# Block products of the last two pairs at other points of pair 1's outputs, and GpSimd's differences of x behind a partial sum

## The chip, the cores and the metric

The kernel runs on one core of one Trainium2 chip. The metric is the device time of the whole program in microseconds (us). The engines are TensorE (PE, matmuls), VectorE (DVE, elementwise work, 32x32 transposes, reductions), ScalarE (ACT, activations and copies), GpSimd (POOL, elementwise work and some DMA issues) and SyncE (SP, DMA issues). Each engine runs its own instructions in program order and waits for the others through semaphores.

## The reference

Eight samples of 512 tokens with 256 features, each with 64 context rows; three experts; everything in float32. The part that matters:

```
nx       = layer_norm(x) * gamma + beta
q, k, v  = nx @ Wq, context @ Wk, context @ Wv
weights  = softmax(q k^T / 16)                       # over the 64 context rows
evidence = weights @ v
combined = [nx, evidence, anchor]                    # 3 x 256 features
probs    = softmax(combined @ router_W + router_b)   # 3 experts
h        = silu(combined @ e_w1 + e_b1)              # 3 x 512
routed   = sum over experts of probs * (h @ e_w2 + e_b2)
g        = sigmoid(silu(combined @ gate_w1 + gate_b1) @ gate_w2 + gate_b2)
out      = x + g * (routed @ out_w + out_b)
```

The kernel never forms `evidence`. It multiplies v with the evidence rows of the first-layer weights ("v and W", the tile `vw`), and then applies the softmax weights to that product.

## The kernel before

**Pairs.** The eight samples are taken in four pairs j = 0 to 3. A pair goes through `gate_layer(j)` (the head of the first layer), `half_layers(j)` (the first layers of gate and experts, in an order written out by hand in `SLOTS`), and `outputs(j)` (second gate layer, experts' second layer, gating, stores). Products are done as seven block products instead of eight (Winograd's scheme), with sums and differences of blocks made beforehand and added afterwards. `combine_x(j)` makes the differences of x for that: four subtractions of 128x512, on GpSimd for pairs 1 to 3 (line 682).

**Order.** All engines' instructions are in program order (`manual_schedule(engines=None)`). While pair j is in `outputs`, the next pair is prepared: the main loop puts steps into `between`, a list for each named point ("begin", "P1", "P8", "P5", "P6", "P2", "P7", "P3", "P4"), and `outputs` calls `run(point)` at these places. Between the points stand the experts' products (`experts`, twelve matmuls of 512 columns each) and the output steps: `keep` (add a partial sum from PSUM to a row sum, line 1418), `subtract` (blocks of h, line 1402), `finish` (three DVE steps, lines 1432 to 1434, one GpSimd addition of x, line 1435, and the stores). For j < 3 the order is: experts u, `keep` r11, P1, experts z, `subtract`, `keep` r22, P8, `subtract`, P5, experts u, `keep` r12, P6, experts y, `finish` r11, P2, `subtract`, experts u, `finish` r22, P7, experts z, `finish` r12, P3, experts u, `finish` r21, P4. Then comes `gate_layer(j + 1)`, with steps at points 1, 5, 6, 3 and 7 (`within`).

**v and W of the last two pairs.** JS is 2. For pairs 0 and 1, `vw` comes from ordinary products (`value_weights`). For pairs 2 and 3 together it comes from seven block products with rows of v (`block_rows`) and columns of W. Part 0 (experts 0 and 1, blocks of 512 columns) is done in `outputs(1)`, part 1 (expert 2, blocks of 256 columns) in `gate_layer(2)`. `block_columns(part)` holds the blocks of W and the three buffers for differences t1, t2 and t4; `late_difference(part, n)` makes one of four differences on DVE (line 886); `late_product(part, n, ps)` is one block product. `late_values(part, banks)` takes three PSUM banks u, y and z and returns four steps:

- first: product 1 into u, ACT copy (line 912), product 2 into y, DVE addition of y (line 907);
- second: product 6 on top of u, ACT copy (line 918);
- third: product 7 on top of u, product 5 into z, ACT copy of z (line 924), DVE addition of u (line 907);
- fourth: product 4 on top of u, ACT copy (line 929), product 3 on top of z, DVE addition of z (line 907), and for the columns finished `value_differences` (line 836).

Part 0's steps are put at P5, P6, P7 and P3 by `late_start`, which runs at P1, and so stand last in each of these lists. Part 1's differences are at P4, its steps in the gate layer at points 1, 5, 6 and 7.

**Other steps named below.** `scores` (line 691, PE), `exponents` (lines 705 to 719: DVE transpose, ACT copy of the logits, DVE maximum and scaling, ACT exponentials), `softmax` (lines 735 and 736, DVE), `evidence_logits` (lines 755 and 758, DVE), `router_logits` (lines 764 to 770, DVE), `turn_weights` (lines 743 and 745, DVE transposes), `router_exp` (line 776, ACT), `gpsimd_behind(column)` (line 125: GpSimd copies one column, and so waits for whoever writes it).

Of the kernel before, what the change touches and what calls it, by code (L numbers as in the profile page):

```python
# [16 lines left out]
def kernel(  # L17
# [53 lines left out]
    B, T, H = x.shape  # L71
# [28 lines left out]
    def bank(i, name):  # L100
        ps = psum.tile([P, 512], F32, tag=f"b{i}", name=name)
        bank_of[ps.name] = i
        return ps

    def spares(*banks):
        spare[:] = banks
# [16 lines left out]
    def gpsimd_behind(column):  # L123

        nc.gpsimd.tensor_copy(behind_t, column)
# [163 lines left out]
    mr = const.tile([P, KH, B, CT], F32, tag="mr", name="mr")  # L289
# [206 lines left out]
    ow_sb = const.tile([P, KH, H], F32, tag="ow_sb", name="ow_sb")  # L496
# [336 lines left out]
    def value_differences(j, g):  # L833
        odd = S["vw", j][CT:, g * RH : (g + 1) * RH]
        odd = odd.rearrange("p (q i c) -> p q i c", i=2, c=P)
        nc.vector.tensor_tensor(odd[:, :, 0, :], odd[:, :, 0, :], odd[:, :, 1, :], ALU.subtract)
# [3 lines left out]
    JS = NP - 2  # L840
    late_v = {}
# [19 lines left out]
    def block_columns(part):  # L861

        if part not in late_v:
            if part == 0:
                c0, n = 0, RH
                t4 = const.tile([P, RH], F32, tag="late_t4", name="late_t4")
                late_v["t4"] = t4
                ts = ow_sb.rearrange("p k n -> p (k n)"), mr[:, :, : B // 2, :], t4
            else:
                c0, n = 2 * RH, RH // 2  # L870
                ts = ow_sb[:, 0, :], ow_sb[:, 1, :], late_v["t4"][:, :n]
            w = [
                [w1[:, KH + k, c0 + i * n : c0 + (i + 1) * n] for i in range(2)] for k in range(KH)
            ]
            late_v[part] = w, ts
        return late_v[part]
# [12 lines left out]
    def late_product(part, n, ps, start=False):  # L889

        ((b11, b12), (b21, b22)), ts = block_columns(part)
        t1, t2, t4 = (t.rearrange("p k b c -> p k (b c)") if len(t.shape) > 3 else t for t in ts)
        rhs = {1: b11, 2: b21, 3: b22, 4: t4, 5: t1, 6: t2, 7: b12}[n]
        product(like(ps, rhs), block_rows(n), rhs, start)

    def late_homes(part):
        (c0, n) = (0, RH) if part == 0 else (2 * RH, RH // 2)
        first, second = S["vw", JS], w1[:, KH, :]
        return [a[:, c0 + i * n : c0 + (i + 1) * n] for a in (first, second) for i in range(2)]

    def late_values(part, banks):

        n = RH if part == 0 else RH // 2
        u, y, z = (bank(i, f"ps_late_{m}")[:, :n] for i, m in zip(banks, "uyz"))

        def plus(dst, ps):
            nc.vector.tensor_tensor(dst, dst, ps, ALU.add)

        def first():
            c11 = late_homes(part)[0]  # L910
            late_product(part, 1, u, True)
            nc.scalar.copy(c11, u)
            late_product(part, 2, y, True)
            plus(c11, y)

        def second():
            late_product(part, 6, u)
            nc.scalar.copy(late_homes(part)[1], u)

        def third():  # L920
            c22 = late_homes(part)[3]
            late_product(part, 7, u)
            late_product(part, 5, z, True)
            nc.scalar.copy(c22, z)
            plus(c22, u)

        def fourth():
            late_product(part, 4, u)
            nc.scalar.copy(late_homes(part)[2], u)
            late_product(part, 3, z)  # L930
            plus(late_homes(part)[1], z)
            for g in (0, 1) if part == 0 else (2,):
                value_differences(JS, g)

        return first, second, third, fourth

    GROUPS = (NE // 2, *range(NE // 2))
# [399 lines left out]
    def outputs(j, steps):  # L1337
        last = j == NP - 1

        def run(point):  # L1340
            for step in steps.get(point, ()):
                step()
# [15 lines left out]
        t2, t3, t4 = gate_sums.pop(j)  # L1358
        g1, g2, g22 = scratch_x("r11"), scratch_x("r12"), scratch_x("r22")
        u, z, y = (bank(i, f"ps_g{n}_{j}") for n, i in (("u", 0), ("z", 2), ("y", 4)))  # L1360
# [26 lines left out]
        def experts(ps, lhs, k, i, start=False):  # L1387
            for q in range(NQ):
                product(ps, lhs(q), hidden(j, q, k, i), start=start and q == 0)

        def combo(s):
            return lambda q: w2s[:, s, q, :]
# [24 lines left out]
        def keep(r, ps):  # L1417
            nc.vector.tensor_tensor(r, r, ps, ALU.add)
# [32 lines left out]
        def finish_late(r, ps, i, row):  # L1451
# [5 lines left out]
        r11, r22, r12, r21 = (  # L1457
            bias_sum(f"r{i + 1}{row + 1}", i, row) for i, row in ((0, 0), (1, 1), (0, 1), (1, 0))
        )
        ug = u  # L1460
        u, y, z = (bank(i, f"ps_{n}2_{j}") for i, n in ((1, "u"), (3, "y"), (5, "z")))
# [10 lines left out]
        run("P5")  # L1472
        experts(u, combo(S2), 0, 1)
        keep(r12, u)
        run("P6")
        if j + 1 < NP:
            experts(y, lambda q: a(q, 0, 1), 1, 0, start=True)
# [53 lines left out]
    with tc.manual_schedule(engines=None):  # L1531
# [77 lines left out]
        def end_setup():  # L1609
# [3 lines left out]
                anchor_columns(g)  # L1613
            value_differences(0, 2)

        for j in range(NP):


            within, between = {}, {}

            def put(where, n, step, *args):
                where.setdefault(n, []).append(lambda: step(*args))

            spares(7, 5)
            if j == 0:
                spares(4, 5, 1)
                copies = []

                def value_product(g):
                    value_weights(0, g, lambda *args: copies.append(args), False)  # L1630

                def copy_values():
                    nc.scalar.copy(*copies.pop(0))

                put(within, 1, value_product, 0)
                put(within, 1, begin_softmax)
                put(within, 5, copy_values)
                put(within, 6, load_table, AF.Silu)
                put(within, 3, value_product, 1)
                put(within, 3, copy_values)  # L1640
                put(within, "sums", end_softmax)
                put(within, 7, value_product, 2)
                put(within, 7, copy_values)
                put(within, 7, end_setup)
            elif j < JS:
                put(within, 3, value_weights, j, 1, nc.scalar.copy, False)
            elif j == JS:
                for point, step in zip((1, 5, 6, 7), late_values(1, (6, 5, 7))):
                    put(within, point, step)
            if j + 1 < NP:  # L1650
                b0, b1 = 2 * j + 2, 2 * j + 3
                if j + 2 < NP:
                    put(between, "begin", load_x, b0 + 2)
                    put(between, "begin", load_x, b1 + 2)
                put(between, "begin", transpose_blocks, b0)
                put(between, "gate", regroup_x, b1)
                put(between, "begin", value_weights, j + 1, E)
                put(between, "begin", store_router_rows, j + 1)
                put(between, "begin", spread_router_rows, j + 1)
                put(between, "P8", transpose_blocks, b1)  # L1660
                put(between, "P6", scores, j + 1)
                put(between, "P6", exponents, j + 1)
                put(between, "P6", combine_x, j + 1, nc.gpsimd)
                if j + 1 < JS:
                    put(between, "P6", value_weights, j + 1, 2)
                elif j + 1 == JS:

                    def late_start():
                        for point, step in zip(("P5", "P6", "P7", "P3"), late_values(0, (0, 2, 4))):
                            put(between, point, step)  # L1670

                    put(between, "P1", late_start)
                    for n in range(4):
                        put(between, "P4", late_difference, 1, n)
                put(between, "P7", softmax, j + 1)
                if j + 1 < JS:
                    put(between, "P7", value_weights, j + 1, 0)
                elif j + 1 > JS:
                    put(between, "P7", value_differences, j + 1, 0)
                    put(between, "P3", value_differences, j + 1, 1)  # L1680
                put(between, "P7", evidence_logits, j + 1)
                put(between, "P7", router_logits, j + 1)
                put(between, "P3", turn_weights, j + 1)
                put(between, "P3", router_exp, j + 1)
            gate_layer(j, within)
            half_layers(j)
            outputs(j, between)


# [32 lines left out]
```

## Time and profile before

| | |
|---|---|
| time, median of 3 runs | 461.32 us (460.79 to 463.81) |
| time of the profiled execution | 463.05 us |
| its span, first to last instruction | 461.2 us |
| mean granted TensorE clock | 0.996 |
| `outputs(1)`, start of the second gate layer to pair 2's gate layer | 199.04 to 255.13 us |
| `gate_layer(2)` up to the first half product | 255.13 to 265.17 us |

The busy time of an engine is the union of its instructions' spans. A matmul's record is longer than the step from one to the next, since they are pipelined: paces are taken from start to start. In a timeline, instructions of one kind in a row are merged into one line with their count, and the bracket at the end has the idle time of the engine before them and what ended it. Both sides of a line are named by tiles: `ps_late_u`, `ps_late_y` and `ps_late_z` are the three banks of the block products.

### The profile page before, as it was taken

The page shows a single profiled execution, that of the slowest core. Times are in us where ns is not written, and L with a number is a line of the kernel's source. Part 1 is how long each engine was busy: PE and PEld are TensorE (multiplying, and loading weights), DVE is VectorE, ACT ScalarE, POOL GpSimd, SP SyncE. Part 2 cuts the span into 40 slices and gives each one's busy share as a digit, 9 for nine tenths or more (in the row PEclk, how much of TensorE's full clock was granted, in tenths as well). Part 3 has the DMA queues.
Part 4 walks back from the last instruction along what each step waited for, and adds up shares of the span by engine and source line. Part 5 has one row for each costly group of instructions (what it writes and reads, how often), then busy time and mean ns, then how long its engine had stood idle before and what let it go on. Part 6 is the DMA issues. An engine that isn't in the chain of part 4 may idle for free.

```text
span 461.2 us, 5521 instructions
## 1 busy us (share of the span) xinstructions
PE 451.3 (98%) x1801; PEld 215.5 (47%) x1801; DVE 368.7 (80%) x698; ACT 214.5 (47%) x378; POOL 99.7 (22%) x149
## 2 busy tenths in 40 slices
PE   8999999999999999999997899999999999999996
PEld 6554445754444444444443444444444444444445
DVE  2878989949698998879798599857989947677983
ACT  3545875463402675474410267547440265658000
POOL 5456600342622200001521120000262220000010
PEclk9999999999999999999998999999999999999999
DMA  8975582363012478003012137500302183000004
GB/s 261 387 154 125 89 248 36 60 125 41 1 28 40 150 155 158 19 1 49 3 23 46 23 98 183 87 1 1 50 2 46 30 207 40 1 0 0 1 16 76
DMA packets 119380, 35.32 MB, mean 77 GB/s; under 512 B 106012, under 2 KB 116312, under 8 KB 118840
## 3 DMA queue, kind: packets, MB, share of 16 engines
q1 hardware_dynamic: 115344, 27.02, 28.7%
q0 software_dynamic: 2080, 7.16, 4.6%
q10 hardware_dynamic: 1928, 0.80, 0.7%
q8 instruction: 14, 0.23, 0.2%
q14 instruction: 14, 0.11, 0.1%
HBM read 27.56 MB, written 7.39 MB: 76 GB/s over the span
## 4 chain that ended last, share of the span: by engine, by line
PE 89%; DVE 5%; DMA 3%; POOL 1%; issue 0%; SPq 0%; DVEq 0%; POOLq 0%
PE ps_u L944 40%; PE ps_z L944 18%; PE ps_y L944 13%; PE ps_gu L944 3%; PE ps_vw L822 3%; PE ps_w2o L547 2%; DMA pb<-pd 2%; PE ps_s L691 2%; PE ps_gz L944 1%; PE ps_tokens L944 1%; PE ps_late_u L944 1%; DMA scr_ctx<-in_ctx_dram 1%; DVE h L1402 1%; PE ps_v L356 1%; PE ps_m L356 1%; PE ps_gy L944 1%
## 5 line engine op out<-in xcount | busy, mean ns | idle before, releaser
L944 PE MATMUL ps_u<-nxT,w 64*128 64x512 f32 (+1 forms) x208 | 96.7, 591 | 0.0
L1023 DVE TENSOR_TENSOR h<-h,pb 128x512 f32<-128x512 f32 x96 | 62.6, 685 | 16.7 <-ACT h L980 10.8
L944 PE MATMUL ps_u<-h,w2o 128*128 128x512 f32 x144 | 64.5, 597 | 0.0
L980 ACT ACTIVATE h<-h,abias 128x512 f32<-128x512 f32 x72 | 49.1, 717 | 30.5 <-DVE h L986 30.4
L944 PE MATMUL ps_y<-nxT,w 64*128 64x512 f32 (+1 forms) x104 | 51.6, 590 | 0.0
L944 PE MATMUL ps_z<-nxT,ws 64*128 64x512 f32 (+1 forms) x104 | 51.5, 591 | 0.0
L944 PE MATMUL ps_z<-T,ws 64*128 64x512 f32 (+1 forms) x104 | 51.5, 590 | 0.0
L1435 POOL TENSOR_TENSOR yb<-yb,xb 128x512 f32<-128x512 f32 x14 | 20.7, 1481 | 138.4 <-DVE yb L1434 125.3
L944 PEld LDWEIGHTS ps_u<-nxT,w 64*128 64x128 f32 (+1 forms) x208 | 37.3, 187 | 26.0 <-issue 22.9
L944 PE MATMUL ps_u<-T,ws 64*128 64x512 f32 (+1 forms) x104 | 49.4, 589 | 0.0
L944 PE MATMUL ps_u<-T,w 64*128 64x512 f32 x112 | 48.3, 590 | 0.0
L944 PEld LDWEIGHTS ps_u<-h,w2o 128*128 128x128 f32 x144 | 27.7, 193 | 33.7 <-issue 33.4
L944 PE MATMUL ps_z<-h,w2s 128*128 128x512 f32 x96 | 42.5, 592 | 0.0
L944 PE MATMUL ps_z<-wT,vw 64*128 64x512 f32 x78 | 39.2, 590 | 0.0
L989 ACT COPY h<-ps_u 128x512 f32<-128x512 f32 x48 | 27.7, 579 | 21.2 <-PE ps_u L944 20.1
L1402 DVE TENSOR_TENSOR h<-h,h 128x1024 f32<-128x1024 f32 x24 | 37.4, 1611 | 0.0
L944 PEld LDWEIGHTS ps_z<-h,w2s 128*128 128x128 f32 x96 | 18.2, 190 | 23.0 <-issue 22.0
L944 PEld LDWEIGHTS ps_y<-nxT,w 64*128 64x128 f32 (+1 forms) x104 | 19.4, 187 | 12.7 <-issue 12.4
L944 PEld LDWEIGHTS ps_z<-T,ws 64*128 64x128 f32 (+1 forms) x104 | 19.2, 187 | 12.5 <-issue 11.3
L944 PEld LDWEIGHTS ps_z<-nxT,ws 64*128 64x128 f32 (+1 forms) x104 | 19.0, 187 | 12.7 <-issue 9.8
L944 PEld LDWEIGHTS ps_u<-T,ws 64*128 64x128 f32 (+1 forms) x104 | 18.4, 187 | 13.2 <-issue 12.3
L944 PEld LDWEIGHTS ps_u<-T,w 64*128 64x128 f32 x112 | 18.3, 187 | 13.0 <-issue 12.3
(271 smaller groups left out, 850.3 us busy)
## 6 DMA issues: line engine op xcount, KB each, us to landing
pb<-pd POOLq DMA_DIRECT2D x4, 1536.0 KB, 6.8
xb<-in_x_dram SPq DMA_DIRECT2D x64, 64.0 KB, 2.4
out_dram<-yb SPq DMA_DIRECT2D x56, 64.0 KB, 1.9
x<-in_x_dram SPq DMA_DIRECT2D x24, 128.0 KB, 3.0
xd<-x SPq DMA_DIRECT2D x24, 128.0 KB, 2.5
xg<-xd SPq DMA_DIRECT2D x48, 64.0 KB, 2.2
w<-in_L_xcond_e_w_dram SPq DMA_DIRECT2D x4, 512.0 KB, 6.9
scr_wa<-in_L_xcond_e_w_dram SPq DMA_DIRECT2D x3, 512.0 KB, 9.4
```

The costliest lines, as they stand in the source:

```text
L356: nc.tensor.matmul(ps, w_sb[:, k, m * P : (m + 1) * P], src[:, k, :], start=(k == 0), stop=(k == KH - 1))
L547: nc.tensor.matmul(ps[:, d * H : (d + 1) * H], w2["T"][u % 2][:, c : c + P], ow_sb[:, k, :], start=(k == 0), stop=(k == KH - 1),)
L691: nc.tensor.matmul(ps[side(i, h), g * NH : (g + 1) * NH], mr[:, k, 2 * j + i, g * TB : (g + 1) * TB], S["nxT", 2 * j + i][:, k, h * NH : ( ...
L822: nc.tensor.matmul(ps, vT[:, k, j * 2 * CT : (j + 1) * 2 * CT], w1[:, KH + k, n0:n1], start=(k == 0), stop=(k == KH - 1),)
L944: return nc.tensor.matmul(ps, lhsT, rhs, start=start, stop=True, skip_group_check=not start)
L980: nc.scalar.activation(h, h if src is None else src, AF.Silu, bias=abias[:, c, 2 * j + i : 2 * j + i + 1])
L989: nc.scalar.copy(chunk(n, i, d), part)
L1023: nc.vector.tensor_tensor(h, h, S["pb", j][:, i, :, 2 * q // RC, :], ALU.mult)
L1402: nc.vector.tensor_tensor(d, p, m, ALU.subtract)
L1435: nc.gpsimd.tensor_tensor(yb, yb, S["xb", 2 * j + row][:, i, :], ALU.add)
```

## The change

Three things change.

1. In `outputs(1)`, the second step of part 0 stands ahead of pair 2's scores instead of at the end of P6; the third step's products and copy stand between scores and exponents at P6 instead of at the end of P7, and its DVE addition behind the exponents' DVE steps (the third step now returns it as a function); the fourth step stands at the end of P7 instead of at the end of P3. The first stays at P5. In `gate_layer(2)` the third step of part 1 is called with its addition at once.
2. Part 1's four differences are at the beginning of P3, ahead of `turn_weights`, instead of at P4. Their t4 lies in `mr` (a 128x256 part that pairs 0 and 1 used) instead of in the buffer of part 0's t4.
3. In every pair's `outputs`, GpSimd copies a column of r12 after `keep(r12, u)`, ahead of P6, so that `combine_x` comes behind that partial sum.

```diff
@@ block_columns
                 t4 = const.tile([P, RH], F32, tag="late_t4", name="late_t4")
-                late_v["t4"] = t4
...
-                ts = ow_sb[:, 0, :], ow_sb[:, 1, :], late_v["t4"][:, :n]
+                ts = ow_sb[:, 0, :], ow_sb[:, 1, :], mr[:, 0, : B // 2, :].rearrange("p b c -> p (b c)")
@@ late_values, third
             late_product(part, 5, z, True)
             nc.scalar.copy(c22, z)
-            plus(c22, u)
+            return lambda: plus(c22, u)
@@ outputs
         experts(u, combo(S2), 0, 1)
         keep(r12, u)
+        gpsimd_behind(r12[:, 0:1])
         run("P6")
@@ main loop
+        late = []
         for j in range(NP):
...
             elif j == JS:
-                for point, step in zip((1, 5, 6, 7), late_values(1, (6, 5, 7))):
-                    put(within, point, step)
+                first, second, third, fourth = late_values(1, (6, 5, 7))
+                put(within, 1, first)
+                put(within, 5, second)
+                put(within, 6, lambda third=third: third()())
+                put(within, 7, fourth)
...
                 put(between, "P8", transpose_blocks, b1)
+                if j + 1 == JS:
+                    put(between, "P6", lambda: late[1]())
                 put(between, "P6", scores, j + 1)
+                if j + 1 == JS:
+                    put(between, "P6", lambda: late.append(late[2]()))
                 put(between, "P6", exponents, j + 1)
+                if j + 1 == JS:
+                    put(between, "P6", lambda: late.pop()())
                 put(between, "P6", combine_x, j + 1, nc.gpsimd)
...
                     def late_start():
-                        for point, step in zip(("P5", "P6", "P7", "P3"), late_values(0, (0, 2, 4))):
-                            put(between, point, step)
+                        late[:] = late_values(0, (0, 2, 4))
 
                     put(between, "P1", late_start)
+                    put(between, "P5", lambda: late[0]())
                     for n in range(4):
-                        put(between, "P4", late_difference, 1, n)
+                        put(between, "P3", late_difference, 1, n)
...
                 put(between, "P7", router_logits, j + 1)
+                if j + 1 == JS:
+                    put(between, "P7", lambda: late[3]())
                 put(between, "P3", turn_weights, j + 1)
```

## The prediction

> **What bounds the kernel now.** I read the page first, then the list of waits of TensorE (PE), then busy time and clock in stretches around those waits, then the timelines of PE, VectorE (DVE) and GpSimd (POOL) there. The page:
>
> ```profile
> span 461.2 us, 5521 instructions
> ...
> PE 451.3 (98%) x1801; PEld 215.5 (47%) x1801; DVE 368.7 (80%) x698; ACT 214.5 (47%) x378; POOL 99.7 (22%) x149
> ...
> PEclk9999999999999999999998999999999999999999
> ```
>
> PE is busy 98%: the change moves PE work and takes none away, so it can gain only what PE loses in waits and at a lower clock; the one low clock digit lies in slice 22 (242.1 to 253.7 us). The waits of PE, microseconds, times, longest:
>
> ```profile
> PE ps_late_u L944 <- DVE w L907: 2.9, 1, 2.9
> PE ps_late_u L944 <- DVE ow_sb L886: 1.5, 1, 1.5
> ```
>
> The two long waits inside the kernel are both on the block products that the change touches. PE's timeline there (start, duration, [idle before]):
>
> ```profile
> 238.21 5.31 PE L944 MATMUL ps_z<-h,w2s 128*128 128x512 f32 x12
> ...
> 246.46 1.41 PE L944 MATMUL ps_late_u<-late_t,vT 128*128 128x512 f32 x2 [2.94 <-DVE w L907]
> ...
> 255.13 1.02 PE L944 MATMUL ps_u<-nxT,w 128*128 128x512 f32 x2
> ...
> 256.86 1.02 PE L944 MATMUL ps_z<-T,ws 128*128 128x512 f32 x2
> ...
> 259.41 0.67 PE L944 MATMUL ps_late_u<-ow_sb,vT 128*128 128x256 f32 x2 [1.53 <-DVE ow_sb L886]
> ...
> 265.17 0.69 PE L944 MATMUL ps_y<-wT,vw 64*128 64x512 f32 x1
> ```
>
> and stretches (busy times, then granted clock):
>
> ```profile
> 243.40:246.46 3.06, 0.12 (x1) 0.00 (x0) 2.82 (x9) 0.22 (x1) 0.00 (x0) 1.00 0.26 44
> 246.46:250.00 3.54, 3.54 (x5) 1.50 (x6) 3.37 (x6) 0.58 (x1) 1.27 (x1) 0.60 0.00 0
> 250.00:253.00 3.00, 3.00 (x8) 1.30 (x7) 2.37 (x6) 0.00 (x0) 0.00 (x0) 0.90 0.51 87
> ...
> 259.40:265.20 5.80, 5.79 (x20) 3.35 (x20) 1.98 (x5) 1.68 (x4) 0.00 (x0) 1.00 0.27 47
> ```
>
> Pace at full clock: twelve 512-column instructions from 205.25 to 210.40, 5.15 us, so 0.43 each and 0.86 for a block product (two instructions; half of it with 256 columns). PE's loss:
> - Product 4 of part 0 could start at 238.21 + 5.15 = 243.36 and starts at 246.46: 3.10.
> - From 246.46 to 255.13, 8.67 us, it runs 16 instructions worth 6.87. The granted clock there was 0.60, then 0.90, after the wait: 1.80.
> - Product 6 of part 1 could start at 256.86 + 0.86 = 257.72 and starts at 259.41: 1.69. Then 5.72 us instead of 5.59: 0.13, at a clock of 1.00.
>
> Sum 6.7 us. That is all there is to gain here; pairs 0 and 2 have no such wait in their outputs.
>
> Why PE waits, in DVE's timeline:
>
> ```profile
> 219.57 5.61 DVE L1402 TENSOR_TENSOR h<-h,h 128x1024 f32<-128x1024 f32 x3
> ...
> 231.55 0.69 DVE L1432 TENSOR_TENSOR r<-r,ps_y 128x512 f32<-128x512 f32 x1 [3.24 <-PE ps_y L944]
> ...
> 240.34 1.77 DVE L736 TENSOR_TENSOR w<-w,rs 128x512 f32<-128x512 f32 x1
> ...
> 245.73 0.68 DVE L907 TENSOR_TENSOR w<-w,ps_late_u 128x512 f32<-128x512 f32 x1
> ...
> 255.33 0.69 DVE L1432 TENSOR_TENSOR r<-r,ps_u 128x512 f32<-128x512 f32 x1 [2.87 <-PE ps_u L944]
> ...
> 257.89 1.37 DVE L886 TENSOR_TENSOR ow_sb<-w,ow_sb 128x256 f32<-128x256 f32 x1
> ```
>
> and of line 1402 alone from 219 to 226 us (shortest, median and longest ns):
>
> ```profile
> L1402 DVE TENSOR_TENSOR h<-h,h x3: 1182/2291/2293, 219.6 to 222.9; 128x1024 f32<-128x1024 f32 x3
> ```
>
> The third step's addition (245.73) stands in DVE's queue behind softmax and evidence; product 4 writes the bank that it reads. Part 1's differences (257.89) stand behind the last output's steps, though DVE had idled 2.87 us just before. The last row: DVE's two-input subtracts take 1.18 alone and 2.29 beside POOL's differences of x (POOL at 219.99 and 221.96, 1.89 and 2.14).
>
> **The change, part by part**, from the profiled execution (span 461.2, time 463.05, so 1.85 around it; it lies 1.73 above the median of the three runs, 461.32).
>
> *Third step at P6.* Products 7 and 5, 1.72 of PE, move from after the experts of "P7" to before ps_y; product 6 only trades places with the scores. No PE work is added, but everything from ps_y to the softmax slides 1.72: DVE's 231.55 becomes 233.27. ACT's copies of the second and third step stand ahead of the copy of the logits, and that one waits for product 5: products at 223.37 (6), scores 224.23 to 226.09, products 7 and 5 to 227.81, ACT's copy (0.58) to 228.5, logits' copy 0.2, DVE's maximum and scaling 1.0 to 229.7, the addition 0.7 to 230.4. DVE had been idle there (3.24 before 231.55), so this costs nothing up to 233.27; beyond, it would go one for one into DVE's queue. The exponentials, 2.8 us in all, end at about 232.7 instead of 231.3, and the softmax asks for them at 241.9. Product 4 then finds its bank read 8 us early: the 3.10 goes, and with it the 1.80 of low clock.
>
> *Fourth step at P7.* Product 4 at 238.2, product 3 to 239.9, experts to 245.1 and 250.2: pair 2's gate layer begins at 250.2 instead of 255.13. Their subtract ends at 238.16 + 1.72 = 239.9, and its first third is enough to start. On DVE the fourth step (250.98 to 252.46, 1.4 net of overlap) moves in front of the r12 output.
>
> *Part 1's differences at P3, ahead of the turning of the weights.* What is late next is DVE's queue, which now has no gap from 233.27 on. Durations are today's: up to the router's logits 247.45 (245.73 + 1.72); fourth step 1.40, 248.85; r12 output 2.13 (246.33 to 248.46), 250.98; differences 2.39 (257.47 to 259.86, a POOL addition beside them in both cases), 253.37, the second of them done at 252.77; turning 2.52 (248.46 to 250.98), 255.89; r21 output 2.14 (255.33 to 257.47), 258.03; part 1's two additions 0.41 each, 258.85. PE from 250.23: product 6 of part 1 is due at 252.81 and its difference is ready at 252.77, so the 1.69 goes; product 4 of part 1 is due at 257.54 and its bank is read at 258.85: a new wait of 1.3. Both ends: none if DVE gains 1.3 somewhere, 3.1 with a low clock as today if it is 1.8 later. I take 1.3, worked out from rows with the same neighbours.
>
> After a wait of 1.69 the clock stayed 1.00 (259.40 to 265.20), after 3.10 it fell to 0.60. 1.3 lies near the first, so I add nothing for the clock.
>
> The Trainium skill, "TensorE: Matmul & The Clock Gate", Part 1, says that the clock is judged in free-running windows of about 3.4 us, which would make the drop after a wait of 3.1 us depend on where a window falls. By that the 1.80 would be lost in some executions only, and the gain in the others would be 3.6.
>
> *Another t4 for part 1* (a quarter of mr that pairs 0 and 1 used): same instruction, same size; nothing. Product 4 of part 0 no longer shares a buffer with it. *Pair 2's gate layer*: the third step's function is called at once, so the order is the same.
>
> *GpSimd behind the partial sum.* One copy of a 128x1 column, then combine_x, in pairs 0 to 2 (pair 3 gets the copy alone). POOL's differences would start at about 224.5 instead of 219.99 and end by about 230 (1.27 to 1.34 each without a neighbour: rows at 224.98 and 226.28). Behind the waiting copy stand only they and the outputs' additions, the first at 235; their reader is the next gate layer, 20 us later. DVE's three subtracts shrink from 5.61 to about 3.4. PE waited for none of it, so 0 for the time; the price if the cover goes is in the slow rival. The small copy's length is not in the trace: between 0.1 (the smallest POOL memset seen) and 1.3, and neither matters. In P6 beside POOL now run a PSUM transpose, a maximum and additions from PSUM, and additions from PSUM took 0.67 beside POOL at 225.10.
>
> The Trainium skill, "SBUF — State Buffer", section "SBUF: two separate sides", says that GpSimd holds it for a whole instruction against DVE's two-input and two-port forms. By that the small scaling at L717 could be held up to 1.3, which DVE's gap before 233.27 hides; the sum would not change.
>
> Sum: -3.10 - 1.80 - 1.69 - 0.13 + 1.3 = -5.4: 463.05 - 5.4 = 457.65 for that execution, 461.32 - 5.4 = **455.9** on the median, 1.2% less.
>
> **Rivals.**
> 1. *DVE's queue is shorter than I add up*: no new wait, -6.7, 454.6. For: I count each POOL neighbour at today's price. Against: the queue is full. 0.10.
> 2. *The new wait lowers the clock*: -5.4 + 1.8 = -3.6, 457.7. Against: the 1.69 row. 0.15.
> 3. *The wait has only moved*: DVE 1.8 later than my sum, product 4 of part 1 waits 3.1 and the clock falls: -6.7 + 4.9 = -1.8, 459.5. For: 25 us of queue without a gap. 0.12.
> 4. *Slower*: combine_x comes beside the r11 output and the subtract after it. Four two-input steps each pay 1.1 (2.29 less 1.18): DVE +4.4, the new wait 5.7, the clock 1.8, together 7.5 against 6.7 lost now: +0.8, 462.1. It decides if POOL starts after about 228, so that its 5 us reach 233.3. Against: the partial sum is due at 224.3. 0.05.
>
> **How the numbers follow.** My forecast has 0.58. Range 454.5 to 459.5: from no new wait to the moved wait; about 0.1 lies outside, with 0.5 us of scatter on either side. 1% (4.6 us, about what a measurement tells from no change) divides at 456.7: the forecast lies 0.8 below it. Faster: 0.50 of the forecast's 0.58 and rival 1, 0.60. Slower by over 1% needs more than rival 4: 0.03. Within 1%: 0.37.
>
> **What would show it.** Right: no wait of ps_late_u on L907 near 238, clock 1.00 from 238 to 260, pair 2's gate layer near 250, a wait of about 1.3 on L907 near 258, L1402 beside no L682. Wrong: a wait over 2.5 us near 258 or a clock below 0.9 after it; a wait for ps_late at 223 to 228 (then ACT's copies are the bound); POOL's L682 after 231.

## The result, and the profile after

The changed kernel takes 458.01 us (median of 6, 457.04 to 458.82) against 461.56 for the kernel before in the same comparison (median of 6): ratio 0.9916, 95% interval 0.9889 to 0.9943. Repeated beside 10 executions of before, it took 458.44 (median of 6) against 462.85: 0.9903, 0.9886 to 0.9920. It is faster by close to 1%, inside the range and on the side that was forecast, but by 3.6 and 4.4 us, less than the forecast 5.4.

The page of the profiled execution (458.82 us):

```profile
span 456.8 us, 5532 instructions
...
PE 450.8 (99%) x1801; PEld 220.0 (48%) x1801; DVE 363.6 (80%) x698; ACT 214.5 (47%) x378; POOL 95.2 (21%) x153
...
PEclk9999999999999999999999999999999999999999
```

The digit 8 of the clock is gone. Lines 868 to 1474 of the program are one lower than before: 907 is now 906, 886 is 885, 1402 is 1401. The waits of PE:

```profile
PE ps_wake L316 <- DVE warm_t L195: 1.1, 1, 1.1
PE ps_late_u L943 <- DVE w L906: 0.9, 1, 0.9
PE ps_u L943 <- DVE h L985: 0.3, 1, 0.3
```

Both long waits (2.9 on line 907, 1.5 on line 886) are gone, and a new one of 0.9 stands on the addition of u. PE's timeline shows where:

```profile
240.30 5.31 PE L943 MATMUL ps_z<-h,w2s 128*128 128x512 f32 x12
245.45 5.31 PE L943 MATMUL ps_u<-h,w2o 128*128 128x512 f32 x12
250.60 1.02 PE L943 MATMUL ps_u<-nxT,w 128*128 128x512 f32 x2
...
252.32 1.02 PE L943 MATMUL ps_z<-T,ws 128*128 128x512 f32 x2
253.40 0.67 PE L943 MATMUL ps_late_u<-ow_sb,vT 128*128 128x256 f32 x2
...
257.35 1.02 PE L943 MATMUL ps_u<-nxT,w 128*128 128x512 f32 x2
259.31 0.70 PE L943 MATMUL ps_late_u<-mr,vT 128*128 128x256 f32 x2 [0.94 <-DVE w L906]
...
260.37 0.69 PE L943 MATMUL ps_y<-wT,vw 64*128 64x512 f32 x1
```

The experts follow each other at full pace (5.15 us from start to start), pair 2's gate layer starts at 250.60, and product 4 of part 1 starts at 259.31 where 257.35 + 0.86 = 258.21 was possible: 1.10 lost. Product 6 of part 1 starts at 253.40 where 252.32 + 0.86 = 253.18 was possible: another 0.22. DVE's timeline has the reason:

```profile
229.25 0.07 DVE L707 MEMSET w<- 128x8 f32 x1 [1.93 <-ACT lg L706]
...
230.15 0.68 DVE L906 TENSOR_TENSOR w<-w,ps_late_u 128x512 f32<-128x512 f32 x1
233.63 0.69 DVE L1431 TENSOR_TENSOR r<-r,ps_y 128x512 f32<-128x512 f32 x1 [2.81 <-PE ps_y L943]
...
251.88 1.38 DVE L885 TENSOR_TENSOR ow_sb<-w,ow_sb 128x256 f32<-128x256 f32 x1
...
257.90 0.71 DVE L1433 STREAM_TRANSPOSE yb<-r 128x512 f32<-128x512 f32 x1
...
258.85 0.41 DVE L906 TENSOR_TENSOR w<-w,ps_late_u 128x256 f32<-128x256 f32 x1
```

DVE waits at 229.25 for ACT's copy of the logits, which stands behind the copy of z, and at 233.63 for the experts; both waits are hidden. From 233.63 until line 906 of part 1 at 258.85 it waits for nothing: the queue is now what PE waits for. The second difference of part 1 (251.88) ends at 253.26, which is what product 6 waits for. GpSimd's timeline, the copy and the four differences behind it, without a neighbour that slows them:

```profile
224.65 0.18 POOL L125 COPY behind_t<-r 128x1 f32<-128x1 f32 x1 [5.63 <-DVE r L1417]
224.79 1.28 POOL L682 TENSOR_TENSOR T<-nxT,nxT 128x512 f32<-128x512 f32 x1
...
228.60 1.27 POOL L682 TENSOR_TENSOR T<-nxT,T 128x512 f32<-128x512 f32 x1
```

Starts of three instructions in PE's timeline split the two profiled executions into stages (us):

| | before | after | difference |
|---|---|---|---|
| start to pair 1's second gate layer | 199.04 | 199.36 | +0.32 |
| from there to pair 2's first half product | 66.13 | 61.01 | -5.12 |
| from there to the end of the span | 196.03 | 196.43 | +0.40 |
| time less span | 1.85 | 2.02 | +0.17 |
| time of the profiled execution | 463.05 | 458.82 | -4.23 |

The stretch that was changed gained 5.12, against 5.4 forecast. The first and the third row move about as much between traces whatever the kernel: in the twelve executions profiled later, pair 1's second gate layer begins between 198.04 and 199.28 us, and from pair 2's second gate layer to pair 3's it is 99.76 to 100.51 us in all fourteen (99.76 before, 100.08 here). The row "time less span" comes back below, with GpSimd's copy. What is left to explain is why the medians show only 3.6.

### The profile page after: what moved, and what is told of

Read it like the earlier page. It is cut to its first block, busy times and chain, and to the rows that moved or that the text cites. A ratio compares the mean times of both kernels' runs of the same rounds, so it can differ in the third digit from the quotient of the medians.

```text
span 456.8 us, 5532 instructions
## 1 busy us (share of the span) xinstructions
PE 450.8 (99%) x1801; PEld 220.0 (48%) x1801; DVE 363.6 (80%) x698; ACT 214.5 (47%) x378; POOL 95.2 (21%) x153
## 4 chain that ended last, share of the span: by engine, by line
PE 87%; DVE 6%; DMA 3%; POOL 1%; issue 1%; ACT 0%; ACTq 0%; DVEq 0%; POOLq 0%
PE ps_u L943 39%; PE ps_z L943 18%; PE ps_y L943 13%; PE ps_gu L943 3%; PE ps_vw L822 3%; PE ps_w2o L547 2%; DMA pb<-pd 2%; PE ps_s L691 2%; PE ps_gz L943 2%; PE ps_tokens L943 1%; DVE h L1401 1%; DMA scr_w<-in_L_xcond_Wk_dram 1%; PE ps_v L356 1%; PE ps_late_u L943 1%; PE ps_m L356 1%; PE ps_gy L943 1%
## 5 line engine op out<-in xcount | busy, mean ns | idle before, releaser
L1401 DVE TENSOR_TENSOR h<-h,h 128x1024 f32<-128x1024 f32 x24 | 30.9, 1342 | 0.0
```

Of the source, the lines that this page charges most:

```text
L1401: nc.vector.tensor_tensor(d, p, m, ALU.subtract)
```

## The experiments

"Theory" in the expectations is DVE's queue as the prediction added it up. Ratios are against the kernel before, run in turn with each group on the same chip.

**The kernel before again.** No edit; the granted clocks of its executions are compared with their times.

> The unchanged kernel once more, for the spread of its executions and the granted clock of each. Measured for the change: 3.6 us by the medians, while the two traces differ by 5.2 us in the stretch that was changed. Theory A (the low clock after the 3.1 us wait is in every execution): all executions show a mean clock near 0.996 and times within about 1 us. Theory B (the clock falls in some executions only, 1.8 us each): two kinds of executions, about 0.996 and slower, about 0.999 or 1.0 and 1.8 us faster, and in the trace either a 0.60 stretch behind the wait or none.

Ratio 1.0005 (0.9986 to 1.0024). The executions of before fall into two kinds by their clock. Over all groups of this study there are 72 of them in turn with the experiments: 53 with a mean clock of 0.993 to 0.996 take 463.0 us on average, 19 with 1.0 take 461.3. So the clock falls in about three of four executions and costs 1.7 us. That it falls behind the 3.1 us wait is seen in the two traces of this kernel, both of the slower kind; none of the faster kind was traced. Theory B holds.

**The steps alone.**

```diff
# the changed kernel, with
-        gpsimd_behind(r12[:, 0:1])
...
-                        put(between, "P3", late_difference, 1, n)
+                        put(between, "P4", late_difference, 1, n)
```

> The second, third and fourth step of part 0 as in the changed kernel, part 1's differences left at P4, no GpSimd copy. Theory A (DVE's queue decides): the 3.1 us wait of product 4 goes, but now part 1's differences stand behind a DVE queue that is later against PE: product 6 of part 1 is due at about 253.2 and its difference ready at about 257.9, a wait of 4.8 us with the clock falling behind it. So only 0.2 to 2.0 us faster than before. Rival (the two waits are independent, each part gains its own): 4.9 us faster.

463.53 us, ratio 1.0031 (1.0015 to 1.0047): slower than before. PE's timeline in this kernel:

```profile
256.74 1.19 PE L943 MATMUL ps_late_u<-ow_sb,vT 128*128 128x256 f32 x2 [4.71 <-DVE ow_sb L885]
257.73 1.91 PE L943 MATMUL ps_y<-nxT,w 128*128 128x512 f32 x2
259.43 1.90 PE L943 MATMUL ps_u<-T,ws 128*128 128x512 f32 x2
```

The wait on the third step's addition is gone and a longer one has come in its place, at the product and with the length that were expected (4.7 against 4.8). Behind it the products run at half pace (1.90 for two that take 1.02). All 12 executions have a clock of 0.996 or less. The rival of independent gains (4.9 us faster) is out; my own lower bound (0.2 faster) was missed by 1.1 us. The low clock came in every execution, where the kernel before has it in three of four, and cost 2.2 us in the trace instead of 1.8.

**The differences alone.**

```diff
# the kernel before, with
-                ts = ow_sb[:, 0, :], ow_sb[:, 1, :], late_v["t4"][:, :n]
+                ts = ow_sb[:, 0, :], ow_sb[:, 1, :], mr[:, 0, : B // 2, :].rearrange("p b c -> p (b c)")
...
-                        put(between, "P4", late_difference, 1, n)
+                        put(between, "P3", late_difference, 1, n)
```

> Only part 1's differences at P3 and their t4 in mr. Both theories: the 1.5 us wait on line 886 goes, the 2.9 us wait on line 907 stays: 1.7 us faster. Theory A adds that steps_only and this one together (1.9 to 3.7) give less than the whole change (5.2 in the traces).

460.88 us, ratio 0.9961 (0.9943 to 0.9978), so 1.8 us (1.0 to 2.6) faster, as expected. The steps lose 0.3%, the differences gain 0.4%, together (the run without GpSimd's copy, below) they gain 1.1%: with the differences at P4, part 1's first user waits for a queue that the earlier steps have not shortened; with the steps late, PE loses 3.1 us ahead of it anyway.

**GpSimd's copy alone.**

```diff
# the kernel before, with
         keep(r12, u)
+        gpsimd_behind(r12[:, 0:1])
```

> Only the GpSimd copy behind the partial sum, in all pairs. Theory: DVE's subtracts fall from 2.29 to 1.2 us in pairs 0 to 2, about 2.2 us of DVE time each, and the time stays, within 0.3 us of before. Rival (DVE is close enough to the bound that its 2.2 us per pair count): up to 2 us faster, from pair 1 where the wait on line 907 ends with DVE's queue.

462.99 us, ratio 1.0007 (0.9991 to 1.0023): the same. Line 1402 in this kernel, pair 1 (shortest, median and longest ns):

```profile
L1402 DVE TENSOR_TENSOR h<-h,h x3: 1185/1217/1222, 219.8 to 222.0; 128x1024 f32<-128x1024 f32 x3
```

The median subtract falls from 2291 to 1217 ns and the time does not move, since both waits of PE stay at 2.9 and 1.5. A cost of a few tenths is not excluded: the time outside the span, from the executions' times and spans, averages 1.92 to 2.00 us in each of the eight kernels with the copy and 1.77 to 1.79 in each of the six without it (here 1.94, before 1.78). The runs do not show why.

**The changed kernel again.**

> The changed kernel once more, beside executions of the kernel before whose clocks are all listed. So far 11 of 35 executions of before had a mean clock of 1.0 and took 461.3 us, 24 had 0.993 to 0.996 and took 462.9: the clock falls behind the 3.1 us wait in two of three, for 1.6 us. Theory B (part of my sum is paid in some executions only): every execution of the changed kernel at 0.998 or more; 5.2 us faster than before's low-clock executions (457.7) and 3.5 faster than its others, so 4.7 against the mean. Rival (a second loss that I have not seen stands somewhere behind the changed stretch): 3.6 us faster against both kinds.

458.44 us, ratio 0.9903 (0.9886 to 0.9920). All 12 executions of the changed kernel in both comparisons have a clock of 0.998 or more; their mean is 458.17. That is 4.9 less than before's low-clock executions and 3.2 less than its others; expected were 5.2 and 3.5. A constant 3.6 against both kinds, the rival, is out. Of the 0.3 that is missing on both, 0.17 is the longer time outside the span (1.95 against 1.78); the rest I have not located.

**Without GpSimd's copy.**

```diff
# the changed kernel, with
-        gpsimd_behind(r12[:, 0:1])
```

> The changed kernel without the GpSimd copy: POOL's differences start at about 220 again and DVE's second subtract costs 2.2 us more. Theory: DVE's gap before the r11 output (2.8 us) swallows it: same as the changed kernel within 0.3 us. Rival (the changed order has made DVE the bound, so its 2.2 us count in full): the wait of product 4 of part 1 grows from 1.1 to 3.3 us, 2.2 to 4 us slower than the changed kernel.

457.49 us, ratio 0.9891 (0.9872 to 0.9909). DVE's subtracts take a median of 2286 ns again, and PE's wait on line 906 is 0.9 as in the changed kernel; the stage takes 60.96 us against 61.01. So DVE's gap swallows it. Expected was the same time within 0.3; the median is 0.95 lower, with overlapping intervals. 0.17 of it lies outside the span, as said above. In the traces the stage is the same, and 1.20 us of the difference between this profiled execution and that of the changed kernel run again is there before the first copy is reached: pair 0's second gate layer begins at 93.49 against 94.69.

**The weights turned later.**

```diff
# the changed kernel, with
                 put(within, 6, lambda third=third: third()())
+                put(within, 6, turn_weights, j)
...
-                put(between, "P3", turn_weights, j + 1)
+                if j + 1 != JS:
+                    put(between, "P3", turn_weights, j + 1)
```

> The changed kernel with pair 2's turning of the weights (2.5 us of DVE) taken out of P3 and put into the gate layer, behind the third step of part 1. Theory (DVE's queue alone makes the new wait of product 4): its bank is read at 256.9 in place of 259.2, product 4 is due at 258.2 and does not wait; the first half products, which read the turned weights, wait at most 0.3. 0.8 to 1.1 us faster than the changed kernel. Rival (product 4 waits for its own chain, not for the queue): no gain, or slower by the delay of the turned weights.

457.37 us, ratio 0.9888 (0.9872 to 0.9904). Product 4 of part 1 no longer waits, and the stage falls from 61.01 to 59.81. But the half layers behind it, 49.12 or 49.13 us to pair 2's second gate layer in every kernel with the turning at P3 and no low clock in them, take 49.98. Between 256 and 264 us the waits of PE's weight loads (PEld) are:

```profile
PEld ps_w L943 <- DVE wT L745: 0.6, 1, 0.6
PEld ps_y L943 <- DVE wT L745: 0.3, 1, 0.3
```

The first half products wait for the turned weights, 0.9 in all where I had allowed 0.3. Net gain in the trace 0.35, not 0.8 to 1.1: the wait was moved, and my estimate of the second queue was off. The median is 1.1 lower than that of the changed kernel, but of the two profiled executions this one is already 1.24 us earlier at pair 0's second gate layer (93.45 against 94.69), where the kernels do not differ.

**The same without the copy.**

```diff
# the weights turned later, with
-        gpsimd_behind(r12[:, 0:1])
```

> turn_later without the GpSimd copy. Theory (the copy has no part in the time; the 0.7 us by which no_gpsimd lay below after_again comes from the wait for pair 0's probabilities, which differs by up to 1 us between executions): same as turn_later, 457.4 within 0.4. Rival (the copy costs some 0.6 us): 456.8 or less.

457.28 us, ratio 0.9883 (0.9863 to 0.9903): same as with the copy; stages 59.75 and 49.99 against 59.81 and 49.98. The copy has no part in the span that the traces show.

**The new wait made longer.** One, two or four reductions on DVE ahead of the addition that product 4 of part 1 waits for; their result is not used.

```diff
# the changed kernel, with (n = 1, 2, 4)
-                put(within, 6, lambda third=third: third()())
+                plus_u = []
+                put(within, 6, lambda third=third: plus_u.append(third()))
+                put(within, 6, idle)       # n reductions of late_t4, 128x512 to 128x8; its body is left out here
+                put(within, 6, lambda: plus_u.pop()())
```

> The changed kernel with one reduction ahead of that addition: a wait of about 1.7 us, the length of the second wait of the kernel before. With two (2.3 us) 5 of 6 executions had the low clock, with none (1.1 us) 0 of 12. Theory (the chance rises with the length of the wait): some executions of 1.7 us have it, one to three of six. Rival (a limit between 1.7 and 2.3 us): none has it and the kernel is 0.6 us slower than the changed one.

> The changed kernel with two reductions of 128x512 (about 0.65 us each, result not used) on DVE ahead of the addition that product 4 of part 1 waits for: a wait of about 2.4 us where the changed kernel has 1.1. If the clock falls by the length of a wait against a window of its own that runs on freely, part of the executions have it (none at 1.7, two of three at 3.1, all of 12 at 4.7), say one of three at 2.4: mean 1.3 plus about 0.5 us slower than the changed kernel, and two kinds of executions. Rival (a fixed limit at about 3 us): clock 1.0 in all, 1.3 us slower.

> The same with four reductions: a wait of about 3.5 us. Theory (the chance rises with the length; 3.1 us in the kernel before had it in 30 of 45): all or all but one have it, mean 0.995 to 0.996, 2.4 + 1.7 = 4.1 us slower than the changed kernel. Rival (the place of the wait in the program counts more than its length): as many as with 2.3 us or fewer, some at 1.0.

458.66, 460.61 and 461.91 us; ratios 0.9908 (0.9892 to 0.9924), 0.9949 (0.9931 to 0.9968) and 0.9980 (0.9963 to 0.9997). With two reductions one execution of three was expected at the low clock, with four all or all but one; the table has what came. It gives the loss at the wait, from start to start in the traces, and all executions whose clock is on record (of before those in turn with the experiments; 9 of 12 in its own run):

| kernel | loss at the wait | executions with a mean clock under 0.998 |
|---|---|---|
| changed | 1.10 us | 0 of 12 |
| one reduction | 1.69 | 0 of 6 |
| two reductions | 2.28 | 5 of 6 |
| before | 3.10 (and 1.69 later) | 53 of 72 |
| GpSimd's copy alone | 3.10 (and 1.70 later) | 8 of 12 |
| differences alone | 3.10 | 8 of 12 |
| four reductions | 3.47 | 9 of 12 |
| steps alone | 4.87 | 12 of 12 |

One and two reductions differ by 0.6 us of wait and 1.8 us of time (means 458.58 and 460.33): the clock makes the difference. They ran on different chips, but it is not the chip that spared one reduction: beside it the kernel before had the low clock in 14 of 17 executions. For two reductions, before, in and behind the wait (busy times, then the clock):

```profile
255.00:257.90 2.90, 2.90 (x9) 1.33 (x7) 2.71 (x6) 0.96 (x2) 0.00 (x0) 1.00 0.13 23
257.90:260.07 2.17, 0.05 (x2) 0.01 (x1) 2.17 (x6) 0.00 (x0) 1.26 (x1) 1.00 0.00 0
260.07:261.40 1.33, 1.33 (x4) 0.67 (x4) 0.54 (x1) 0.58 (x2) 0.00 (x0) 0.76 0.56 98
261.40:264.60 3.20, 3.20 (x11) 1.40 (x11) 2.69 (x8) 1.42 (x2) 1.00 (x2) 0.57 0.25 44
264.60:268.00 3.40, 3.40 (x18) 1.52 (x16) 2.23 (x9) 1.58 (x3) 1.69 (x5) 1.00 0.05 9
```

A limit between 1.7 and 2.3 us (the rival of wait_1) fits the short waits. But 2.3 us having it in 5 of 6 and 3.5 in 9 of 12 shows no rise with length; three executions with four reductions still ran at 0.999. Whether place or length decides above 2 us stays open; the last section has an estimate.

**A better version.** Part 0's two `value_differences` at the end of part 1's fourth step, behind the addition that product 4 of part 1 waits for:

```diff
# the changed kernel, in fourth()
-            for g in (0, 1) if part == 0 else (2,):
+            for g in () if part == 0 else (2, 0, 1):
                 value_differences(JS, g)
```

> The changed kernel with part 0's two value_differences (0.76 us of DVE) moved from the end of the fourth step at P7 into the fourth step of part 1, behind the addition that product 4 of part 1 waits for. Theory (DVE's queue alone sets that wait): the wait falls by 0.76, from 1.10 to about 0.35, and the 0.22 before product 6 goes, so the stretch from pair 1's second gate layer to the first half product takes 60.0 us in place of 61.0; the columns are read some 20 slots later, so nothing is given back: about 0.9 us faster than the changed kernel. Rival (as with turn_later, what DVE does later is waited for later): the half layers lengthen by as much.

456.78 us (456.48 to 457.70), ratio 0.9877 (0.9848 to 0.9906), the lowest median of the study. PE's timeline:

```profile
255.91 1.02 PE L943 MATMUL ps_u<-nxT,w 128*128 128x512 f32 x2
257.25 0.70 PE L943 MATMUL ps_late_u<-mr,vT 128*128 128x256 f32 x2 [0.32 <-DVE w L906]
...
258.31 0.69 PE L943 MATMUL ps_y<-wT,vw 64*128 64x512 f32 x1
```

The idle time falls from 0.94 to 0.32, the 0.22 before product 6 goes, the stage falls from 61.01 to 60.09, and the half layers stay at 49.13: this work had a late enough reader. The gain over the changed kernel is read from these stages; the two ran on different chips, and the intervals of their ratios overlap.

## Why the prediction was right, and where it was off

*What PE loses.* Right: 6.7 us in two waits and a stretch of low clock was all there was to gain, and the stretch gained 5.12 of it. In the sum a small slip: from 259.41 to 265.17 it is 5.76, not 5.72, so 0.17 in place of 0.13 and 6.76 in all.

*Third step at P6.* Right in each step: ACT's copies delay the logits, DVE idles there, the addition ends at 230.8 (230.4 forecast), y's outputs slide to 233.63 (233.27), product 4 runs at once. Shown: the 2.9 us wait for part 0's addition is in every trace with the step at P7 and in none with it at P6.

*Fourth step and differences.* Right: pair 2's gate layer at 250.60 (250.2), the differences beside GpSimd's addition at 1.38 (1.37 before), the additions of part 1 done at 259.26 (258.85), a new wait of 1.10 (1.3). That the queue alone makes it is shown from both sides: reductions put in lengthen it by 0.6 each, 0.76 us taken out shortens it by 0.62. Two small terms were put at nothing: product 6 still lost 0.22, and from its start to the first half product PE took 6.97 us, of which 1.10 is the new wait and 5.59 the work, so 0.28 more. PE's loss is then 1.60 after, against 6.76 before, which is the 5.12 of the stretch but for 0.04.

*GpSimd behind the partial sum.* Right for the span: nothing, and shown alone, left out, and left out of another version. Outside the span it goes with 0.17 us that the sum did not have. The 1.18 for a subtract "alone" was read from one that ran from 219.57 to 220.75 and had GpSimd beside it from 219.99; the number stands, since three without a neighbour take 1.19 to 1.22. The small scaling at L717 ran at 230.06, behind GpSimd's last difference (done at 229.87), so this trace does not show whether it could have been held.

*The rivals.* No new wait: wrong by 1.1 us. A low clock behind it: in none of 12 executions. The moved wait and the slower one: neither; GpSimd's differences ended at 229.9, before the 233.3 that would have decided the last.

*What was off* is the size of one term and what it was set against. "From 246.46 to 255.13 ... 1.80" was read from one execution and taken in full, but the kernel before pays it in 53 of 72 executions, 1.7 us each: 1.25 on average. I had cited the Trainium skill ("TensorE: Matmul & The Clock Gate", Part 1) for windows that run freely, had drawn from it that the drop would come in some executions only, and then left that out of the sum; the runs agree with it here, 19 executions of 72 without the drop. And "461.32 - 5.4" started from a median of three executions, which of two kinds 1.7 apart says little: over the 72 later ones the median is 462.8. Set against that, 5.4 would have given 457.4; measured were 458.0 and 458.4.

## What to carry to other kernels

When a step is moved ahead in a full queue, look for who stands last in that queue now: two moves that lose or gain little alone (+0.3% and -0.4% here) gave -1.1% together, because what the steps gained was lost again at the differences, which stood last in the queue. A further DVE step is worth moving past a wait only if its own reader is far: 0.76 us moved to a place still well ahead of its reader was kept, as 0.9 us of the stage; 2.5 us moved in front of the next products came back as 0.9 us of waits. And before a stall is priced from one trace, look at the clock of several executions: what follows the stall may be paid in some of them only.

## What the runs showed of the hardware

A wait of 2.3 us was enough to lower TensorE's clock in 5 of 6 executions; 1.7 us did it in none of 6. For GpSimd's copy alone, whose 3.1 us wait ends at 246.70, and for the steps alone, whose 4.9 us wait ends at 256.74 (busy times, then the clock):

```profile
246.70:248.90 2.20, 2.20 (x4) 1.00 (x5) 2.07 (x4) 0.59 (x1) 0.05 (x1) 0.82 0.00 0
248.90:252.30 3.40, 3.40 (x6) 1.39 (x5) 3.26 (x8) 0.00 (x0) 1.22 (x1) 0.62 0.28 48
252.30:255.00 2.70, 2.70 (x8) 1.20 (x7) 0.39 (x2) 0.00 (x0) 0.00 (x0) 1.00 0.21 36
```

```profile
251.00:256.70 5.70, 1.03 (x3) 0.19 (x1) 5.47 (x10) 0.79 (x2) 1.92 (x2) 0.80 0.27 46
256.70:260.00 3.30, 3.26 (x5) 1.85 (x6) 0.89 (x3) 0.37 (x1) 0.00 (x0) 0.50 0.48 82
260.00:263.00 3.00, 3.00 (x9) 1.62 (x8) 0.36 (x1) 0.96 (x2) 0.00 (x0) 0.80 0.00 0
```

Shorter stretches of these traces have the clock at 1.00 or at 0.50, with the steps between. So a row with 0.82 over 2.20 us had 0.8 us of 0.50, and the first three rows together have 3.4 us of it, from 248.1 to 251.5: the products ran at full pace for 1.4 us after the wait before they slowed. All seven traces with a drop give one length, 3.4 us, and the steps alone twice that, 6.8. At half pace 3.4 us cost 1.7. The start of the low stretch lies 0.4 to 1.4 us behind the end of the wait in five of the seven, but 0.5 us ahead of it in the differences alone, and 2.4 us ahead of it in the steps alone, where 4.5 of the 6.8 us are left to pay: the 2.2.

An estimate from these numbers: in the 3.4 us ahead of each such start PE stood still for 2.0 to 3.0 us. If the clock is decided once in every 3.4 us, by whether PE stood still for about 2.0 of them, then a wait of 1.7 us never lowers it and 4.9 always does, while for 3.1 it depends on how the wait falls across two such stretches: 2.5 of the 3.4 us of possible positions lower it, 74%, and 53 of 72 executions did. The same gives half for 2.3 us (5 of 6 measured) and 84% for 3.5 (9 of 12). No run moved a wait of one length, so this is not shown; nor does it say when a second stretch follows, as in the steps alone (mean clock 0.993) and, by that number, in some executions of before.

The GpSimd differences took 1.27 to 1.28 us each behind the partial sum and up to 2.25 beside DVE's two-input subtracts, which themselves went from 2.29 to 1.22 us: both sides paid for running at the same time, and neither was on the path.
